# Layer 0's score maxima read from SBUF, and a probability chain cut in three, in a two-layer cross-attention kernel

## The chip, the cores and the metric

The kernel runs on one core of a Trainium2 chip. A core has five engines that run their own instruction streams: TensorE (PE, matrix products; its weight loads, PEld, are listed apart), VectorE (DVE), ScalarE (ACT), GpSimd (POOL) and SyncE (SP, which here issues nearly all DMAs). They share SBUF, the working memory. PE writes its products to PSUM[...], which VectorE and ScalarE read. The metric is the time of one execution on the device, in microseconds; lower is better.

## The reference

Two layers of cross-attention in float32 over x of shape (4, 512, 320), with a context of 1024 tokens of width 512, and 20 heads of width 16. In layer 0 the last four context tokens are "ip" tokens with their own weights:

```python
scores_t = einsum('bhsd,bhtd->bhst', q, k_t) * attn_scale     # 1020 text tokens
probs_t  = softmax(scores_t, axis=-1)
text_out = einsum('bhst,bhtd->bhsd', probs_t, v_t)
attn_scores = einsum('bhsd,bhnd->bhsn', q, k_ip) * attn_scale # 4 ip tokens
qsem  = _l2norm(einsum('bhst,bte->bhse', probs_t, text_ehs))
sem   = einsum('bhse,bne->bhsn', qsem, _l2norm(ip_ehs))
probs_ip = softmax(attn_scores + SEM_SCALE * sem, axis=-1) * spatial_mask
out = (text_out + einsum('bhsn,bhnd->bhsd', probs_ip, v_ip)) @ W_out + b_out + residual
```

Layer 1 takes that output as its hidden states. It attends to 77 text tokens and, in a second softmax, to the other 947 tokens, adds both results, projects, and adds bias and residual.

The large term of layer 0 is the norm in `_l2norm`: for each query and head the vector probs_t @ text_ehs of 512 numbers is needed to get the sum of its squares. The kernel gets these vectors with a product scheme of seven block products per pair of heads instead of eight (one Strassen step: blocks "11", "21", "t1", "t2", "22", "t3", "t4").

## The kernel before

**Units of work.** A turn is one batch and one tile of 128 query rows: 16 turns. A turn has five groups of four heads: 80 groups, numbered `gi`. A group has two units, one for each pair of heads. A unit runs `part0` to `part3`, and behind each part there is a stop. So a group has eight stops, k = 0 to 7. At each stop other work is slipped in between the products of layer 0: one piece from the queues `sub`, `late` or `proj` (function `item`), at stops 2, 4, 5 and 6 a step of layer 1, at stop 2 the function `max0` of the next group, and at stops 5 to 7 pieces of the next group's exponentials (`end_stop`).

**The scores of layer 0.** At stops 0 and 1 of group gi, `fill0(gi + 1, k)` makes the next group's scores, half of the context tokens each time (c = 0, then c = 1). `fill` takes two PSUM tiles `sc` of two banks each, one for each pair of heads. 32 small products fill both: four at a time, two into each tile. Then, for each tile, ScalarE copies the scores to an SBUF tile e (line 476), and VectorE takes the maxima over the four context tiles (lines 477 and 478), so that 128 maxima per query are left. The maxima read the PSUM tile. The pool of the `sc` tiles has two of them, and layer 1's scores (`mx`, `ex`) use the same two. So each fill waits until both tiles of the use before are read. Two engines that read one bank are kept apart by the framework, one after the other. For c = 1 the last four tokens are left out of the maxima and the remaining tile is added by two further instructions.

At stop 2 `max0` turns the maxima with PE, finishes them, and sends the negated maxima through DRAM to all partitions (tile `bc`). `do_exp` adds them to e on VectorE, ScalarE takes the exponential (line 710), and GpSimd prepares a difference.

**Products around the fills.** `part0` writes banks b1 and b2; ScalarE copies b1 (tile `p`, line 804), VectorE adds b2 to it (`c`) and ScalarE sums the squares of `c` (`junk`, line 790). `part1` makes a product into bank b3, VectorE copies that (`p5`; the profile leaves out numbers of buffers, so it is `p` as well, on the row of a VectorE COPY `p<-b`), and a second product goes to b1. `part2` accumulates a further product on b3: PE has to wait for the copy `p5`.

**Order.** All of PE's instructions and those of VectorE that go through `vec` are kept in the order of the program. What goes through `nc.vector`, `nc.scalar` and `nc.gpsimd` is placed by the framework's planner, which has a model of times of its own.

**The end of a turn.** Behind the eighth stop of a turn's fifth group `finish` runs. It loads x, and computes the probabilities of the ip tokens: the sums' reciprocal `r`, scaled outputs `o` and similarities `sem`, the squared norm `n2`, its root on ScalarE (`n1`), and then a softmax over four tokens with an Exp on ScalarE (`pe`), 16 VectorE and 2 ScalarE instructions in all. [...]the trace shows table loads at both. VectorE's part goes through `nc.vector`, in one piece. Then `late` gets two empty pieces and four further ones, one for each of the next stops: `turn_ip` (turns `pe` with PE), `add_ip`, `turn_out` and `multiply`, which starts layer 1 of this turn.

Of the kernel before, what the change touches and what calls it, by code (L numbers as in the profile page):

```python
# [14 lines left out]
AF = mybir.ActivationFunctionType  # L15
ALU = mybir.AluOpType
AX = mybir.AxisListType
# [3 lines left out]
P = 128  # L21
B, S, C = 4, 512, 320
T, E = 1024, 512
H, D = 20, 16
NIP = 4
# [15 lines left out]
V0W = D + NIP + 1  # L41
# [5 lines left out]
TH = TT // 2  # L47
# [3 lines left out]
SEM_SCALE = 0.5  # L51
EPS2 = 1e-24
# [3 lines left out]
def xattn_pair(ctx_stack: ExitStack, tc: tile.TileContext, a: dict, out: bass.AP):  # L56
    nc = tc.nc
# [18 lines left out]
    def mm(out, lhsT, rhs, start, stop, on=False):  # L76
        tc.keep_in_program_order(nc.tensor.matmul(out, lhsT=lhsT, rhs=rhs, start=start, stop=stop, skip_group_check=on))  # L77
# [11 lines left out]
    vec = InOrder(nc.vector)  # L89

    def tr(out, in_, ident):
        tc.keep_in_program_order(nc.tensor.transpose(out, in_, ident))  # L92
# [5 lines left out]
    def tp(name):  # L98
        turn_of[0] += 1
        if idle[0] and turn_of[0] % 4:  # L100
            return ps_qs.tile([P, 512], F32, tag=f"qs{turn_of[0] % 4 - 1}", name=name)
        return ps_tp.tile([P, 512], F32, tag="tp", name=name)
# [31 lines left out]
    spat = cst.tile([P, ST], F32, name="spat")  # L134
# [5 lines left out]
    def load_x(b, s, ns, pl, tag):  # L140
        t = pl.tile([P, ns, C], F32, tag=tag, name=f"{tag}_{b}_{s}")
        nc.sync.dma_start(t, a["x"][b, s * P : (s + ns) * P, :].rearrange("(t p) c -> p t c", p=P))
        return t
# [87 lines left out]
    def zero_below(t):  # L231
        nc.gpsimd.memset(t[64:, NC - 1, :], 0.0)
        return t
# [208 lines left out]
    late = deque()  # L442
# [21 lines left out]
    def fill(c, m, name):  # L464


        ps = [ps_sc.tile([P, 2, 512], F32, tag="sc", name=f"sc{name}_{c}_{i}") for i in range(2)]
        for j in range(TH):
            t = (TH * c + j) * P
            for r in range(4):  # L470
                mm(ps[r // 2][:, r % 2, j * P : (j + 1) * P], kq[0][0][32 * r : 32 * r + D, t : t + P],
                   qq[0][0][32 * r : 32 * r + D, :], True, True)
        e = []
        for i in range(2):
            e.append(ep.tile([P, 2, TH, P], F32, tag="e0", name=f"e{name}_{c}_{i}"))
            nc.scalar.copy(e[i].rearrange("p h t s -> p (h t s)"), ps[i].rearrange("p h n -> p (h n)"))  # L476
            vec.tensor_reduce(m[:, c, 2 * i : 2 * i + 2, :],
                                    ps[i][:, :, 0 : (TH - c) * P].rearrange("p h (t s) -> p h s t", s=P), AX.X, ALU.max)
        return e


# [181 lines left out]
    def fill0(gi, c):  # L663
        if gi >= len(G):
            return
        name = f"0_{gi}"
        if c == 0:
            ms[gi] = big.tile([P, 2, 4, P], F32, tag="m0", name=f"m{name}")
        e = fill(c, ms[gi], name)
        for i in range(2):  # L670
            es[gi, i, c] = e[i]
        if c:

            m = ms[gi]
            vec.tensor_tensor(m[:, 0], m[:, 0], m[:, 1], ALU.max)
            for i in range(2):
                x = m[:, 0, 2 * i : 2 * i + 2, :]
                vec.scalar_tensor_tensor(x, x, drop[:, 0:1], e[i][:, :, TH - 1, :], ALU.add, ALU.max)
            if gi + 1 < len(G):
                turn, g = G[gi + 1]  # L680
                load_quad(0, zs[TURNS[turn][0]], turn, g)
# [149 lines left out]
    def finish(turn):  # L831
        b, s = TURNS[turn]
        w, z, name = state.pop(turn), zs[b], f"0_{turn}"

        def small(tag, shape):
            return (st2 if tag in ("pT", "oT") else big).tile(shape, F32, tag=tag, name=f"{tag}_{name}")

        def wide(t, n=NIP):
            return t.unsqueeze(2).to_broadcast([P, H, n])

        z.xr[turn] = xr = load_x(b, s, 1, st3, "xr")
        nc.gpsimd.tensor_tensor(xr, xr, bo[0].unsqueeze(1).to_broadcast([P, 1, C]), ALU.add)
        pv, ss, ips = w["pv"], w["ss"], w["ips"]
        r = small("r", [P, H])
        nc.vector.reciprocal(r, pv[:, :, V0W - 1])
        o = small("o", [P, H, D])
        nc.vector.tensor_tensor(o, pv[:, :, 0:D], wide(r, D), ALU.mult)
        sem = small("sem", [P, H, NIP])
        nc.vector.tensor_tensor(sem, pv[:, :, D : D + NIP], wide(r), ALU.mult)

        n2 = small("n2", [P, H])
        nc.vector.tensor_tensor(n2, ss[:, :, 0], ss[:, :, 1], ALU.add)
        nc.vector.tensor_tensor(n2, n2, r, ALU.mult)
        nc.vector.tensor_tensor(n2, n2, r, ALU.mult)
        nc.vector.tensor_scalar(n2, n2, EPS2, None, ALU.max)
        n1 = small("n1", [P, H])
        nc.scalar.activation(n1, n2, AF.Sqrt)
        rn = small("rn", [P, H])
        nc.vector.reciprocal(rn, n1)
        nc.vector.tensor_tensor(sem, sem, wide(rn), ALU.mult)  # L860
        pe = small("pe", [P, H, NIP])
        nc.vector.scalar_tensor_tensor(pe, sem, SEM_SCALE, ips, ALU.mult, ALU.add)
        mx = small("mx", [P, H])
        nc.vector.tensor_reduce(mx, pe, AX.X, ALU.max)
        nc.vector.tensor_tensor(pe, pe, wide(mx), ALU.subtract)
        nc.scalar.activation(pe, pe, AF.Exp)
        sums = small("sums", [P, H])
        nc.vector.tensor_reduce(sums, pe, AX.X, ALU.add)
        re = small("re", [P, H])
        nc.vector.reciprocal(re, sums)  # L870
        nc.vector.tensor_scalar(re, re, spat[:, s : s + 1], None, ALU.mult)
        nc.vector.tensor_tensor(pe, pe, wide(re), ALU.mult)
        of2, box = o.rearrange("p h d -> p (h d)"), {}

        def turn_ip():
            pt = tp(f"pt_p_{name}")
            tr(pt[: H * NIP, 0:P], pe.rearrange("p h n -> p (h n)"), ident)
            box["pT"] = small("pT", [H * NIP, P])
            vec.tensor_copy(box["pT"], pt[: H * NIP, 0:P])

        def add_ip():
            pt = tp(f"pt_ip_{name}")
            mm(pt[:, 0:C], box["pT"], z.vip, True, True)
            vec.tensor_tensor(of2, pt[:, 0:C], of2, ALU.add)

        def turn_out():
            pt = tp(f"pt_o_{name}")
            for c, (c0, n) in enumerate(CK):
                tr(pt[:n, c * P : (c + 1) * P], of2[:, c0 : c0 + n], ident)
            box["oT"] = zero_below(small("oT", [P, NC, P]))  # L890
            vec.tensor_copy(box["oT"][:, 0:2].rearrange("p c s -> p (c s)"), pt[:, 0 : 2 * P])
            vec.tensor_copy(box["oT"][:64, 2, :], pt[:64, 2 * P : 3 * P])

        def multiply():
            pt = tp(f"pt_y_{name}")
            for c in range(NC):
                mm(pt[:, 0:C], box["oT"][:, c, :], wo0[:, c, :], c == 0, c == NC - 1)
            vec.tensor_tensor(xr[:, 0, :], pt[:, 0:C], xr[:, 0, :], ALU.add)
            layer1(turn)


        late.extend([lambda: None] * 2 + [turn_ip, add_ip, turn_out, multiply])


    z, (turns, scores, layer0, rest) = projections(0)
# [11 lines left out]
    for g in range(HG):  # L917
        for r in range(4):
            c = 64 * g + D * r
# [51 lines left out]
    for gi, (turn, g) in enumerate(G):  # L971
        b, s = TURNS[turn]
        n = gi % NQ
        ending[0] = gi == len(G) - 1
        if n == 1 and b + 1 < B:
            zs[b + 1], steps = projections(b + 1)
            proj.extend(steps)
        if n == NQ - 2:
            while proj:
                proj.popleft()()  # L980
        for i in range(2):
            u = units.pop((gi, i))
            for k, part in enumerate((u.part0, u.part1, u.part2, u.part3)):
                part()
                stop(gi, 4 * i + k)
                if k == 2:
                    ahead(gi + i, 1 - i)
            for c in range(2):
                es.pop((gi, i, c))
        if g == HG - 1:  # L990
            finish(turn)
# [29 lines left out]
```

## Time and profile before

| | before |
|---|---|
| median of 3 runs | 3784.29 us (3783.63 to 3785.22) |
| the profiled execution | 3784.95 us, its span 3783.2 us |
| PE busy | 3547.9 us (94%) |
| PEld busy | 2826.8 us (75%) |
| DVE busy | 2080.8 us (55%) |
| ACT busy | 1498.8 us (40%) |
| POOL busy | 1012.3 us (27%) |
| mean granted PE clock | 0.958 of full speed |
| copies of the scores (line 476) | 320, 1.01 us each |
| DMA queue of SyncE | 30% of 16 engines' span |

The span runs from the first to the last instruction; the execution is longer by 1.75 us. An engine's busy share is an average over the whole span. An idle engine costs nothing unless the others wait for it, so the rows of interest are those that tell what ended an engine's idle time. The clock column tells which share of its full speed PE was granted: it is 1.00 or 0.50 in every stretch.

### The profile page before, as it was taken

To read this page: it belongs to the slowest core of one execution; us is meant where nothing else is said; L and a number is where in the kernel's file an instruction comes from. 1 tells how busy PE (TensorE), PEld (TensorE's weight loads), DVE (VectorE), ACT (ScalarE), POOL (GpSimd) and SP (SyncE) were. 2 spreads that over 40 slices of the span, in tenths; PEclk is the share of its full clock that TensorE was granted. 3 is DMA by queue.
4 is the path that set the end of the run, shared out by engine and by line. 5 is a ranking of instruction groups with operands and counts; after the bars stand their busy time and mean duration, and the time that the engine had idled before them with its cause. 6 is when DMAs were issued, how large, how long until landed. Compare 5 with 4: busy or idle time off the path is not lost.

```text
span 3783.2 us, 74188 instructions
## 1 busy us (share of the span) xinstructions
PE 3547.9 (94%) x29060; PEld 2826.8 (75%) x29060; DVE 2080.8 (55%) x3795; ACT 1498.8 (40%) x2824; POOL 1012.3 (27%) x1039
## 2 busy tenths in 40 slices
PE   7799999999999999999999999999999999999976
PEld 5677777777787777777777787777777777777765
DVE  2344455566554654556665554556665665665544
ACT  1233334344443433434443443444444444444432
POOL 1222222233222222223322222222322322332210
PEclk9899999999999999999999999999999999999986
DMA  6444332222334233222234433222232222222211
GB/s 180 106 125 125 71 83 39 49 39 48 84 87 102 60 97 89 50 63 40 44 80 104 101 69 95 62 58 45 46 79 48 44 41 51 41 44 38 46 34 26
DMA packets 704986, 258.76 MB, mean 68 GB/s; under 512 B 571024, under 2 KB 679024, under 8 KB 704640
## 3 DMA queue, kind: packets, MB, share of 16 engines
q1 hardware_dynamic: 704464, 253.82, 30.0%
q8 instruction: 232, 3.80, 0.4%
q14 instruction: 114, 0.93, 0.1%
q10 hardware_dynamic: 176, 0.20, 0.0%
HBM read 213.51 MB, written 40.33 MB: 67 GB/s over the span
## 4 chain that ended last, share of the span: by engine, by line
PE 79%; DVE 12%; ACT 3%; DMA 3%; issue 2%; SPq 1%; POOL 0%; DVEq 0%; ACTq 0%; POOLq 0%
PE b L77 47%; PE ex L77 6%; PE pv L77 5%; DVE m L87 5%; PE pt_k L77 4%; PE sc L77 4%; DVE e L87 4%; PE mx L77 4%; PE pt_v L77 3%; PE pt_y L77 2%; PE pt_q L77 2%; PE mx L92 1%; ACT e L710 1%; ACT e L476 1%; DVE c L87 1%
## 5 line engine op out<-in xcount | busy, mean ns | idle before, releaser
L77 PE MATMUL b<-xv_t,e 128*128 128x277 f32 x2560 | 675.7, 407 | 1.3 <-DVE c L87 1.3
L77 PE MATMUL b<-xv,e 128*128 128x277 f32 (+1 forms) x2560 | 653.4, 408 | 10.7 <-ACT e L710 10.7
L77 PEld LDWEIGHTS b<-xv,e 128*128 128x128 f32 x2560 | 480.1, 190 | 145.0 <-ACT e L710 10.9
L77 PEld LDWEIGHTS b<-xv_t,e 128*128 128x128 f32 x2560 | 486.8, 195 | 117.4 <-DVE c L87 4.6
L710 ACT ACTIVATE e<-e 128x1024 f32<-128x1024 f32 x320 | 338.2, 1057 | 468.0 <-DVE e L87 467.8
L805 POOL TENSOR_TENSOR e<-e,s 128x512 f32<-128x512 f32 x160 | 223.8, 1398 | 1071.2 <-PE b L77 1071.2
L87 DVE TENSOR_REDUCE m<-sc 128x256 f32<-128x1024 f32 (+1 forms) x320 | 338.0, 1087 | 267.7 <-ACT e L476 267.7
L87 DVE TENSOR_REDUCE m<-mx 128x2 f32<-128x870 f32 (+1 forms) x320 | 363.7, 1137 | 100.9 <-PE ex L77 92.5
L529 ACT ACTIVATE e<-ex 128x1024 f32<-128x1024 f32 x320 | 325.7, 1018 | 235.9 <-PE ex L77 235.9
L790 ACT ACTIVATE junk<-c 128x256 f32<-128x256 f32 x480 | 198.7, 414 | 513.1 <-DVE c L87 505.1
L77 PE MATMUL ex<-qa,kq 19*128 19x128 f32 x5120 | 383.3, 290 | 6.8 <-DVE qa L87 5.9
L77 PE MATMUL mx<-kq,qq 16*128 16x512 f32 x1280 | 365.2, 661 | 21.4 <-DVE m L87 15.2
L476 ACT COPY e<-sc 128x1024 f32<-128x1024 f32 x320 | 307.4, 1012 | 196.0 <-PE sc L77 194.8
L87 DVE TENSOR_TENSOR e<-e,bc 128x1024 f32<-128x1024 f32 x320 | 368.9, 1173 | 9.5 <-DMA bc<-zd 9.5
L77 PE MATMUL b<-xs,e 128*128 128x256 f32 x1280 | 366.8, 436 | 0.0
L712 POOL TENSOR_TENSOR e<-e 128x512 f32<-128x512 f32 x160 | 205.4, 1284 | 594.5 <-ACT e L710 594.4
L87 DVE TENSOR_TENSOR c<-b,p 128x256 f32<-128x256 f32 x320 | 134.1, 419 | 408.0 <-PE b L77 369.2
L77 PEld LDWEIGHTS ex<-qa,kq 19*128 19x128 f32 x5120 | 321.5, 192 | 13.6 <-DVE qa L87 5.4
L77 PE MATMUL b<-xs_t,e 128*128 128x256 f32 x1280 | 319.6, 393 | 8.0 <-POOL e L805 8.0
L77 PE MATMUL sc<-qq,kq 16*128 16x128 f32 x5120 | 221.8, 299 | 93.3 <-DVE m L87 93.3
L77 PE MATMUL b<-xs_t,s 128*128 128x256 f32 x1280 | 303.2, 380 | 2.1 <-ACT p L804 2.1
L77 PEld LDWEIGHTS b<-xs,e 128*128 128x128 f32 x1280 | 259.0, 212 | 56.6 <-issue 4.4
(192 smaller groups left out, 4221.8 us busy)
## 6 DMA issues: line engine op xcount, KB each, us to landing
kq<-kd SPq DMA_DIRECT2D x640, 64.0 KB
v1q<-v1d SPq DMA_DIRECT2D x80, 373.5 KB
bc<-zd SPq DMA_DIRECT2D x80, 256.0 KB
xv<-v0d SPq DMA_DIRECT2D x480, 42.0 KB
xv_t<-v0d SPq DMA_DIRECT2D x320, 42.0 KB
L_xattn_W_k<-in_L_xattn_W_k_dram SPq DMA_DIRECT2D x13, 640.0 KB
L_xattn_W_v<-in_L_xattn_W_v_dram SPq DMA_DIRECT2D x13, 640.0 KB
raw<-in_ctx_dram SPq DMA_DIRECT2D x32, 256.0 KB
```

What stands on the lines that cost most here:

```text
L77: tc.keep_in_program_order(nc.tensor.matmul(out, lhsT=lhsT, rhs=rhs, start=start, stop=stop, skip_group_check=on))
L87: return lambda *args, **kw: keep(getattr(self.engine, name)(*args, **kw))
L92: tc.keep_in_program_order(nc.tensor.transpose(out, in_, ident))
L476: nc.scalar.copy(e[i].rearrange("p h t s -> p (h t s)"), ps[i].rearrange("p h n -> p (h n)"))
L529: nc.scalar.activation(e.rearrange("p i j s -> p (i j s)"), ps.rearrange("p i n -> p (i n)"), AF.Exp)
L710: nc.scalar.activation(flat, flat, AF.Exp)
L712: nc.gpsimd.tensor_tensor(e[:, 1], e[:, 1], e[:, 0], ALU.subtract)
L790: nc.scalar.activation(junk, x, AF.Square, accum_out=self.w["ss"][:, self.h + r, k : k + 1])
L805: nc.gpsimd.tensor_tensor(self.e("11"), self.e("11"), self.s2, ALU.add)
```

## The change

Two edits. In `fill` the maxima read e, the copy in SBUF that ScalarE has just made, and no longer the PSUM tile; the elements and their order are the same. In `finish` the chain is cut in three: `norms` runs at once, `exps` at the next stop and `shares` at the one behind it, in the places of the two empty pieces. All of the chain's VectorE instructions go through `vec` now, so they hold their place in the program's order, and the root's input is computed before `o` and `sem`.

```diff
@@ fill
-            vec.tensor_reduce(m[:, c, 2 * i : 2 * i + 2, :],
-                                    ps[i][:, :, 0 : (TH - c) * P].rearrange("p h (t s) -> p h s t", s=P), AX.X, ALU.max)
+            vec.tensor_reduce(m[:, c, 2 * i : 2 * i + 2, :], e[i][:, :, 0 : TH - c].rearrange("p h t s -> p h s t"), AX.X,
+                              ALU.max)
@@ finish
-        nc.vector.reciprocal(r, pv[:, :, V0W - 1])
-        nc.vector.tensor_tensor(o, pv[:, :, 0:D], wide(r, D), ALU.mult)
-        nc.vector.tensor_tensor(sem, pv[:, :, D : D + NIP], wide(r), ALU.mult)
-        nc.vector.tensor_tensor(n2, ss[:, :, 0], ss[:, :, 1], ALU.add)
...
-        nc.vector.tensor_tensor(pe, pe, wide(re), ALU.mult)
+        def norms():
+            vec.reciprocal(r, pv[:, :, V0W - 1])
+            vec.tensor_tensor(n2, ss[:, :, 0], ss[:, :, 1], ALU.add)
+            vec.tensor_tensor(n2, n2, r, ALU.mult)
+            vec.tensor_tensor(n2, n2, r, ALU.mult)
+            vec.tensor_scalar(n2, n2, EPS2, None, ALU.max)
+            nc.scalar.activation(n1, n2, AF.Sqrt)
+            vec.tensor_tensor(o, pv[:, :, 0:D], wide(r, D), ALU.mult)
+            vec.tensor_tensor(sem, pv[:, :, D : D + NIP], wide(r), ALU.mult)
+        def exps():
+            vec.reciprocal(rn, n1)
+            vec.tensor_tensor(sem, sem, wide(rn), ALU.mult)
+            vec.scalar_tensor_tensor(pe, sem, SEM_SCALE, ips, ALU.mult, ALU.add)
+            vec.tensor_reduce(mx, pe, AX.X, ALU.max)
+            vec.tensor_tensor(pe, pe, wide(mx), ALU.subtract)
+            nc.scalar.activation(pe, pe, AF.Exp)
+        def shares():
+            vec.tensor_reduce(sums, pe, AX.X, ALU.add)
+            vec.reciprocal(re, sums)
+            vec.tensor_scalar(re, re, spat[:, s : s + 1], None, ALU.mult)
+            vec.tensor_tensor(pe, pe, wide(re), ALU.mult)
...
-        late.extend([lambda: None] * 2 + [turn_ip, add_ip, turn_out, multiply])
+        norms()
+        late.extend([exps, shares, turn_ip, add_ip, turn_out, multiply])
```

More of the change, by code (lines that the diff above doesn't have):

```diff
@@ L844, in finish @@
         r = small("r", [P, H])
-        nc.vector.reciprocal(r, pv[:, :, V0W - 1])
         o = small("o", [P, H, D])
-        nc.vector.tensor_tensor(o, pv[:, :, 0:D], wide(r, D), ALU.mult)
         sem = small("sem", [P, H, NIP])
-        nc.vector.tensor_tensor(sem, pv[:, :, D : D + NIP], wide(r), ALU.mult)
         n2 = small("n2", [P, H])
-        nc.vector.tensor_tensor(n2, ss[:, :, 0], ss[:, :, 1], ALU.add)
-        nc.vector.tensor_tensor(n2, n2, r, ALU.mult)
-        nc.vector.tensor_tensor(n2, n2, r, ALU.mult)
@@ L855, in finish @@
-        nc.vector.tensor_scalar(n2, n2, EPS2, None, ALU.max)
         n1 = small("n1", [P, H])
-        nc.scalar.activation(n1, n2, AF.Sqrt)
         rn = small("rn", [P, H])
-        nc.vector.reciprocal(rn, n1)
-        nc.vector.tensor_tensor(sem, sem, wide(rn), ALU.mult)
         pe = small("pe", [P, H, NIP])
-        nc.vector.scalar_tensor_tensor(pe, sem, SEM_SCALE, ips, ALU.mult, ALU.add)
         mx = small("mx", [P, H])
-        nc.vector.tensor_reduce(mx, pe, AX.X, ALU.max)
-        nc.vector.tensor_tensor(pe, pe, wide(mx), ALU.subtract)
@@ L866, in finish @@
-        nc.scalar.activation(pe, pe, AF.Exp)
         sums = small("sums", [P, H])
-        nc.vector.tensor_reduce(sums, pe, AX.X, ALU.add)
         re = small("re", [P, H])
-        nc.vector.reciprocal(re, sums)
-        nc.vector.tensor_scalar(re, re, spat[:, s : s + 1], None, ALU.mult)
-        nc.vector.tensor_tensor(pe, pe, wide(re), ALU.mult)
+        def norms():
[7 more added lines that the diff above has]
+            vec.tensor_tensor(sem, pv[:, :, D : D + NIP], wide(r), ALU.mult)
```

## The prediction

> **What bounds it now.** I read the busy shares first: TensorE (PE) is busy 94% of the span, VectorE (DVE) 55%, ScalarE (ACT) 40%. So the few places where PE stands still decide, and I went to the groups of instructions and their idle time. PE's longest wait by far is in front of the layer-0 score matmuls, and VectorE's maxima of those scores end it:
>
> ```profile
> L87 DVE TENSOR_REDUCE m<-sc 128x256 f32<-128x1024 f32 (+1 forms) x320 | 338.0, 1087 | 267.7 <-ACT e L476 267.7
> ...
> L77 PE MATMUL sc<-qq,kq 16*128 16x128 f32 x5120 | 221.8, 299 | 93.3 <-DVE m L87 93.3
> ```
>
> The last field is idle time and what ended it. The maxima wait for ACT's copy of the same scores: two readers of one bank follow each other, copy first. PE's 93.3 us is two fifths of all that it isn't busy (3783.2 - 3547.9 = 235 us). Going through the timeline fill by fill, all of it is at stop 1 (second fill, c = 1), in 34 of 80 groups: 15 first groups after a turn's end (60.7 us), 18 others (32.3 us), and 0.3 us at the start. An ordinary one:
>
> ```profile
> 2701.52 1.90 ACT L476 COPY e<-sc 128x1024 f32<-128x1024 f32 x2
> ...
> 2702.55 2.35 DVE L87 TENSOR_REDUCE m<-sc 128x256 f32<-128x1024 f32 x2 [1.39 <-ACT e L476]
> ...
> 2703.82 0.49 PE L77 MATMUL sc<-qq,kq 16*128 16x128 f32 x4 [1.08 <-DVE m L87]
> 2704.82 0.41 DVE L87 COPY p<-b 128x256 f32<-128x256 f32 x1
> ...
> 2704.96 1.16 PE L77 MATMUL sc<-qq,kq 16*128 16x128 f32 x28 [0.64 <-DVE m L87]
> ...
> 2706.05 3.17 PE L77 MATMUL b<-xs,e 128*128 128x256 f32 x8
> ```
>
> PE was ready at 2702.74 and got through the fill at 2706.05, 3.31 us later. Note the p copy of part1 (p5, bank b3) right behind the maxima. The chain of waits runs through just such places.
>
> **Maxima, price of one.** 1.216 us for 1024 elements, 0.957 for 768[...]. From SBUF no large reduce is in the trace. Near rows: the SBUF pair m<-m, 512 elements, 692 ns[...]; a SBUF shuffle of 256 takes 438 ns, 442 beside GpSimd, so one input doesn't queue behind GpSimd. I take the same price.[...] Here each element lies 512 bytes after the last[...]. The rows for a strided and a contiguous read of 20 elements:
>
> ```profile
> L845 DVE RECIPROCAL r<-pv x16: 263/266/278, 369.8 to 3645.3; 128x20 f32<-128x20 f32 x16
> ```
> ```profile
> L859 DVE RECIPROCAL rn<-n x16: 262/278/280, 374.0 to 3648.1; 128x20 f32<-128x20 f32 x16
> ```
>
> A step of 84 bytes costs nothing (266 against 278 ns median[...]). The row decides[...].
>
> **Maxima, what is gained.** The banks come free when the second copy ends, 2703.42, not at 2704.90. The fill runs 2703.47 to 2704.60. Then the next product, b<-xs,e into b3, needs the p copy to have read b3, and that copy stands in VectorE's fixed order behind both maxima: 2705.23. So b starts at 2705.29, not 2706.05: 0.76 us, half of what the wait suggests. **The wait moves, from sc to b behind the p copy.** The same arithmetic (fill start = later of ready and copy end; b start = later of fill + 1.13 and p copy end + 0.06) for each of the 33: 16.0 us over the 18 ordinary ones, 23.2 us over the 15 turn ends, together 39. In the other 46 groups the p copy is early by at least 0.43 us, nothing changes.
>
> **Clock.** A stall costs twice here: after it PE runs at half clock.
>
> ```profile
> 2706.70:2710.10 3.40, 3.40 (x10) 2.59 (x9) 2.93 (x4) 1.28 (x2) 0.00 (x0) 0.50 0.25 68
> 2742.30:2745.70 3.40, 3.40 (x27) 2.76 (x29) 2.69 (x3) 1.73 (x3) 1.18 (x1) 1.00 0.03 8
> ```
>
> These are stretches of the stalled group and of its neighbour; the column before the last two is the granted clock.[...] By the trace 12 of the 15 are followed by 3.4 us at 0.50, 1.7 us lost each, 20 us in all; the trace decides. Afterwards such a group idles 0.73 + 0.64 = 1.37 us. Single stalls of 1.27, 1.28 and 1.38 us kept the clock (at 701.6, 2010.2, 602.9), one of 1.51 lost it (2315.2). I take 8 of the 12 as saved: 13 us, ends 0 and 20.
>
> **The chain.** Same 16 x (16 DVE, 2 ACT) instructions, no DMA moved. Now at a turn's end (ACT alone):
>
> ```profile
> 2819.67 1.28 ACT L857 ACT_TABLE_LOAD   x1
> 2820.97 0.22 ACT L857 ACTIVATE n<-n 128x20 f32<-128x20 f32 x1
> 2821.20 1.28 ACT L866 ACT_TABLE_LOAD   x1
> 2822.96 0.27 ACT L866 ACTIVATE pe<-pe 128x80 f32<-128x80 f32 x1 [0.48 <-DVE pe L865]
> 2823.14 1.91 ACT L476 COPY e<-sc 128x1024 f32<-128x1024 f32 x2
> ```
>
> VectorE runs the chain from 2818.21 to 2824.36, 1.55 us of it waiting for the root, and only then c and pv of part0, the maxima and the p copy (to 2827.37). The copies, whose scores were ready at 2818.1, stand behind both table loads. After: norms (1.5 us) to 2819.7 or so, c and pv to 2820.5 while the root loads; rn waits until 2821.2, exps end near 2822.9; shares (1.1 us) go behind the p copy and are hidden, as VectorE waits over 2 us there for the second fill. The new wait blocks the maxima behind rn; they need the copies anyway. What ACT does is open, since its order isn't kept: the Exp may stand before the two copies (copies end 2825.3, p copy 2827.2: 0.2 us better than the maxima alone give), between them (2826.95: 0.45 us), or behind (copies end 2823.7, maxima from 2822.95, p copy 2825.75: 1.65 us). The middle is likeliest: PE issues sc right behind the product that c reads, so the scores are there about when c is, and the Exp needs another 1.3 us of VectorE. The second wait, of shares for the Exp (ended by 2825.3 in each order), has the second fill's maxima behind it, which come later anyway. 15 x 0.45 = 7 us; ends 3 and 25. The loads: a Copy directly behind the root (at 372 us) needed none; for a Square no row tells, so 0 to 16 x 1.28 = 20 us; I take 0, since the Exp reloads anyway. PE's idle at turn ends stays near 4 us, and so do most of the 6.8 us half-clock stretches; I count 3 of 15 shortened by 1.7: 5 us, up to 25 in the good order. At the very end the qa add no longer stands behind the chain (PE waited 3.63 us there at 3648 to 3652): 2 us.
>
> **Sum.** 39 + 13 + 7 + 5 + 2 = 66. The profiled execution took 3784.95 us (span 3783.2 and 1.75 around), the median is 3784.29: 3784.3 - 66 = 3718.
>
> **Rivals.**
> - Copies before the Exp at turn ends: 39 + 20 + 25 + 25 + 2 = 111, 3673. For: scores ready 5 us before they are copied. Against: Exp comes first in the program. Chance 0.2.
> - The wait only moves: b stalls behind the p copy, the clock drops as before, the chain gives nothing; 39 alone, 3745. For: total idle per stalled group falls only from 1.73 to 1.37. Against: the three stalls that kept the clock. 0.22.
> - Slower:[...] It decides from 0.59 us more per maximum (39 / 33 / 2). The rows at 84 bytes[...] speak against. With its milder forms, and a square that reloads tables: 0.12.
> - No change, gain given back at turn ends: 0.03.
> - The forecast: 0.43, its own range 3700 to 3735.
>
> 0.2% is 7.6 us, about what can be told from no change. Faster 0.85, same 0.03, slower 0.12. The range leaves out the slow case and the best tail: 3664 to 3768.
>
> **What would show it.** Right: sc no longer idle behind DVE m but, for about a third of the time, behind ACT e; a new b <- DVE p wait of some 0.6 us in 30 places; maxima from e still at 1.2 and 0.96 us; the rn wait (18.6 us) smaller; fewer 0.50 stretches. Wrong: a maximum over 1.8 us, half-clock time not below 290 us (321 now), copies at turn ends later than 5 us behind the scores, or more than 32 table loads in the chain.

## The result, and the profile after

| | before | after |
|---|---|---|
| median, 11 runs each | 3784.29 us (3781.61 to 3792.54) | 3806.94 us (3792.76 to 3815.05) |
| the profiled execution, span | 3784.95, 3783.2 us | 3792.76, 3790.7 us |
| clock in the profiled execution | 0.958 | 0.960 |

The changed kernel is slower: 1.0055 times the time before, 95% interval 1.0041 to 1.0068. That is 21 us more, where 66 us less had been forecast. The profiled execution of after is the quickest of its eleven. The other ten show granted clocks from 0.952 to 0.958, so the trace explains the first 8 us of the loss. The rest goes with the clock, though no trace of those ten is kept: at a mean of 0.955 PE spends 9% of the time at half speed, at 0.960 8%. One per cent of 3800 us is 38 us at half speed, and 19 us of work lost.

The page of after, busy row and groups by line (busy us, mean ns | idle before it, what ended it):

```profile
PE 3526.4 (93%) x29060; PEld 2813.5 (74%) x29060; DVE 2198.0 (58%) x3795; ACT 1501.1 (40%) x2824; POOL 1014.4 (27%) x1039
...
L87 DVE TENSOR_REDUCE m<-e 128x256 f32<-128x1024 f32 (+1 forms) x320 | 459.4, 1476 | 169.8 <-ACT e L476 168.8
...
L77 PE MATMUL b<-xs,e 128*128 128x256 f32 x1280 | 360.1, 430 | 81.8 <-DVE p L87 55.6
```

VectorE executes the same 3795 instructions and is busy 117 us longer. The maxima alone take 121 us more, 459.4 against 338.0. With the two shapes kept apart, first before, then after:

```profile
L87 DVE TENSOR_REDUCE m<-sc 128x256 f32<-128x1024 f32 x160 | 188.3, 1218 | 106.1 <-ACT e L476 106.1
L87 DVE TENSOR_REDUCE m<-sc 128x256 f32<-128x768 f32 x160 | 149.7, 957 | 161.5 <-ACT e L476 161.5
```
```profile
L87 DVE TENSOR_REDUCE m<-e 128x256 f32<-128x1024 f32 x160 | 301.5, 1926 | 123.5 <-ACT e L476 123.5
L87 DVE TENSOR_REDUCE m<-e 128x256 f32<-128x768 f32 x160 | 157.9, 1027 | 46.3 <-ACT e L476 45.3
```

A maximum over four tiles takes 1.93 us from SBUF, where it took 1.22 from the bank; over three tiles it takes 1.03 instead of 0.96. So the loss is in one of the two shapes, and it isn't a general price of SBUF.

PE's waits of after (us in total, times, longest):

```profile
PE b L77 <- DVE p L87: 55.6, 43, 3.5
PE sc L77 <- ACT e L476: 27.9, 40, 2.0
PE b L77 <- DVE sums L87: 21.7, 12, 2.1
...
PE b L77 <- ACT p L804: 10.7, 9, 1.2
```

The wait of sc for the maxima (93.3 us) is gone, and a wait of sc for ACT's copies is left at 30% of it. But the product b behind the p copy now waits 77 us, the first and third rows together. The third row names `sums`, the first instruction of the chain's third piece. It is the same place at turn ends: VectorE's copy stands right ahead of `sums` there, and PE begins 0.10 us after the copy, before `sums` ends. Releasers are inferred, and one looks at the times before believing a name:

```profile
2834.69 0.42 DVE L87 COPY p<-b 128x256 f32<-128x256 f32 x1
2835.02 0.23 DVE L87 TENSOR_REDUCE sums<-pe 128x20 f32<-128x80 f32 x1
...
2835.21 3.75 PE L77 MATMUL b<-xs,e 128*128 128x256 f32 x8 [1.60 <-issue]
```

The ordinary group that the prediction worked through, on the timeline of after (start, duration, engine, idle before it):

```profile
2707.19 1.89 PE L77 MATMUL b<-xs_t,s 128*128 128x256 f32 x8
...
2707.86 1.91 ACT L476 COPY e<-sc 128x1024 f32<-128x1024 f32 x2
2708.89 3.74 DVE L87 TENSOR_REDUCE m<-e 128x256 f32<-128x1024 f32 x2 [1.39 <-ACT e L476]
...
2709.82 1.16 PE L77 MATMUL sc<-qq,kq 16*128 16x128 f32 x28 [0.32 <-ACT e L476]
...
2712.55 0.41 DVE L87 COPY p<-b 128x256 f32<-128x256 f32 x1
...
2713.11 3.32 PE L77 MATMUL b<-xs,e 128*128 128x256 f32 x7 [2.12 <-DVE p L87]
```

The fill gets its banks at once, 0.32 us late instead of 1.73. Then PE stands 2.12 us before b. From being ready for the fill (2709.08, the end of the first row) to the start of b it takes 4.03 us, where it took 3.31. The products of b last 3.3 us, where eight take 2.0 at full speed; the stretch behind the stall shows a granted clock of 0.50 (the column before the last two):

```profile
2713.60:2716.40 2.80, 2.80 (x8) 2.20 (x7) 2.73 (x5) 0.00 (x0) 0.00 (x0) 0.50 0.26 54
```

I measured this interval in all 80 groups of both traces. The 18 ordinary stalled groups lose 8.5 us in sum. Of the 46 groups without a stall before, 25 now have one, of 0.71 us in the median: 16.8 us. The 15 turn ends gain 20.0, the first group 0.7. Together 4.5 us are lost. The wait for ACT's copy p adds 8.6 us (10.7 against 2.1), and half-speed time falls from 320.8 to 308.6 us, worth some 6. That makes 7 us, about the 7.5 between the two spans.

ACT at a turn's end, after:

```profile
2824.66 1.06 ACT L710 ACTIVATE e<-e 128x1024 f32<-128x1024 f32 x1 [3.24 <-DVE e L87]
2825.74 1.28 ACT L863 ACT_TABLE_LOAD   x1
2827.03 0.22 ACT L863 ACTIVATE n<-n 128x20 f32<-128x20 f32 x1
2827.16 0.37 ACT L804 COPY p<-b 128x277 f32<-128x277 f32 x1
...
2828.55 1.28 ACT L873 ACT_TABLE_LOAD   x1
2829.84 0.27 ACT L873 ACTIVATE pe<-pe 128x80 f32<-128x80 f32 x1
2830.02 1.91 ACT L476 COPY e<-sc 128x1024 f32<-128x1024 f32 x2
```

Both loads still stand ahead of the copies of the scores. New is that the copy p of part0, which PE's next product needs, now stands behind the root's load. The copies begin 5.6 us behind their scores in 10 of the 15 turn ends, where 5.0 was the rule before.

### The profile page after: what moved, and what is told of

Its sections match the earlier page's. It is cut to its first block, busy times and chain, and to the rows that moved or that the text cites. A ratio compares the mean times of both kernels' runs of the same rounds, so it can differ in the third digit from the quotient of the medians.

```text
span 3790.7 us, 74186 instructions
## 1 busy us (share of the span) xinstructions
PE 3526.4 (93%) x29060; PEld 2813.5 (74%) x29060; DVE 2198.0 (58%) x3795; ACT 1501.1 (40%) x2824; POOL 1014.4 (27%) x1039
## 4 chain that ended last, share of the span: by engine, by line
PE 72%; DVE 15%; ACT 5%; DMA 3%; issue 3%; SPq 1%; POOL 0%; ACTq 0%; DVEq 0%; POOLq 0%
PE b L77 45%; DVE m L87 8%; PE ex L77 6%; PE pv L77 5%; DVE e L87 4%; PE pt_k L77 4%; PE mx L77 4%; PE pt_v L77 3%; PE pt_y L77 2%; ACT e L476 2%; PE sc L77 2%; PE mx L92 1%; ACT e L710 1%; PE pt_q L77 1%; ACT junk L790 1%
## 5 line engine op out<-in xcount | busy, mean ns | idle before, releaser
L87 DVE TENSOR_REDUCE m<-e 128x256 f32<-128x1024 f32 (+1 forms) x320 | 459.4, 1476 | 169.8 <-ACT e L476 168.8
L77 PE MATMUL b<-xs,e 128*128 128x256 f32 x1280 | 360.1, 430 | 81.8 <-DVE p L87 55.6
L77 PE MATMUL b<-xs_t,s 128*128 128x256 f32 x1280 | 304.2, 380 | 10.7 <-ACT p L804 10.7
L77 PEld LDWEIGHTS b<-xs_t,s 128*128 128x128 f32 x1280 | 243.3, 191 | 48.0 <-ACT p L804 14.7
```

The source lines that it names most:

```text
L87: return lambda *args, **kw: keep(getattr(self.engine, name)(*args, **kw))
```

## The experiments

The first question was what brings the loss: the price of the strided maximum, which the p copy queued behind two of them pays twice, or the order in which VectorE and ACT now do their work. Ratios are to the runs of the kernel before on the same chip.

**Each edit alone.** The first kernel has only the edit in `fill`:

```diff
-            vec.tensor_reduce(m[:, c, 2 * i : 2 * i + 2, :],
-                                    ps[i][:, :, 0 : (TH - c) * P].rearrange("p h (t s) -> p h s t", s=P), AX.X, ALU.max)
+            vec.tensor_reduce(m[:, c, 2 * i : 2 * i + 2, :], e[i][:, :, 0 : TH - c].rearrange("p h t s -> p h s t"), AX.X,
+                              ALU.max)
```

> Only the first edit: maxima from SBUF, the chain as before. Theory 'price' (a maximum over four tiles costs 1.92 us from SBUF and 1.22 from the banks, and the p copy that PE waits for stands behind two of them): slower than before by 20 to 45 us, since the ordinary groups lose 25.8 us as in the changed kernel and the turn ends gain next to nothing without the split chain. Theory 'order' (the chain held in program order is what costs): 35 to 70 us faster than before, as forecast for the maxima alone.

The second has only the edit in `finish`:

```diff
+        norms()
+        late.extend([exps, shares, turn_ip, add_ip, turn_out, multiply])
```

> Only the second edit: chain in three pieces, maxima from the banks. Theory 'price': faster than before by 20 to 60 us, as the turn ends gain (19.8 us in the changed kernel in spite of the dear maxima, 15 x 1.4 us more without them) and the ordinary groups are as before. Theory 'order': slower than before, by 10 to 40 us.

The maxima alone: 3814.3 us, ratio 1.0080 (1.0067 to 1.0092), 30 us slower. The chain alone: 3768.0 us, ratio 0.9958 (0.9945 to 0.9972), 16 us faster, a little less than the 20 to 60 expected under "price". So the whole loss is the first edit's. On top of it the second still gives some 9 us (1.0055 for both against 1.0080). PE's waits with the maxima alone:

```profile
PE b L77 <- DVE p L87: 83.3, 55, 3.6
PE sc L77 <- ACT e L476: 37.4, 40, 2.4
```

The two rows make 120.7 us, in place of the 93.3 us of one wait before.

**The same edit with another instruction.** If the price decides, the change's own idea must pay once the maximum is cheap. Here the maxima still read e, in the same place in the order, but as maxima of two tiles at a time; `m[:, 1]` serves as scratch at c = 0.

```diff
-            vec.tensor_reduce(m[:, c, 2 * i : 2 * i + 2, :], e[i][:, :, 0 : TH - c].rearrange("p h t s -> p h s t"), AX.X,
-                              ALU.max)
+            mi = m[:, c, 2 * i : 2 * i + 2, :]
+            if c == 0:
+                h2 = m[:, 1].rearrange("p (h k) s -> p h k s", h=2)
+                vec.tensor_tensor(h2, e[i][:, :, 0:2], e[i][:, :, 2:4], ALU.max)
+                vec.tensor_tensor(mi, h2[:, :, 0], h2[:, :, 1], ALU.max)
+            else:
+                vec.tensor_tensor(mi, e[i][:, :, 0], e[i][:, :, 1], ALU.max)
+                vec.tensor_tensor(mi, mi, e[i][:, :, 2], ALU.max)
```

> The changed kernel, with each maximum from SBUF made of two pairwise maxima over contiguous runs (512 and 256 elements for four tiles, 256 and 256 for three) in place of one strided reduce. Theory 'price': 0.69 + 0.45 = 1.15 us for four tiles, so the p copy comes as early as from the banks or a little earlier; about the forecast, 3690 to 3740 us, and PE's wait for DVE p about 0.6 us in some 30 places. Theory 'order': no faster than 3790 us.[...]

3740.1 us, ratio 0.9887 (0.9874 to 0.9901): 43 us faster than before. One maximum over four tiles takes 0.82 and 0.45 us in the mean, 1.27 together, near the 1.22 from the bank. (The first takes 0.69 us in the median, but 39 of 160 took longer, up to 1.76; what held them up was not tested.) Timeline of an ordinary group:

```profile
2675.16 0.98 DVE L87 TENSOR_TENSOR m<-e 128x512 f32<-128x512 f32 x1 [1.39 <-ACT e L476]
...
2676.10 1.16 PE L77 MATMUL sc<-qq,kq 16*128 16x128 f32 x28 [0.33 <-ACT e L476]
...
2677.77 0.42 DVE L87 COPY p<-b 128x256 f32<-128x256 f32 x1
...
2678.34 1.97 PE L77 MATMUL b<-xs,e 128*128 128x256 f32 x8 [1.08 <-DVE p L87]
```

The wait has moved from sc to b here as well, at 0.33 + 1.08 = 1.41 us in place of 1.73, and b runs at full speed. With the price put right, the sign of the change turns.

**The same maxima, behind the p copy.** This tries the other cause, the place behind which the p copy waits. The maxima keep their slow form, but those of the first fill are put off to stop 1, where they are issued behind part1's p copy.

```diff
+    def maxima(gi, c):
+        for i in range(2):
+            vec.tensor_reduce(ms[gi][:, c, 2 * i : 2 * i + 2, :],
+                              es[gi, i, c][:, :, 0 : TH - c].rearrange("p h t s -> p h s t"), AX.X, ALU.max)
...
+        if c == 0:
+            owed.append(gi)
...
+            while owed:
+                maxima(owed.pop(), 0)
+            maxima(gi, 1)
...
+        if k == 1 and owed:
+            maxima(owed.pop(), 0)
```

> The changed kernel, the strided maxima of a group's first fill put behind part1's p copy in VectorE's order (at the start of stop 1). Theory 'price': the dear maxima stand in nobody's way up to the turning of the maxima at stop 2, PE's 77 us of waiting for DVE p and sums go, leaving the wait for ACT's copies (28 us): 3690 to 3740 us, unless the turning at stop 2 becomes late. Theory 'order': no faster than 3790 us.

3721.1 us, ratio 0.9835 (0.9821 to 0.9848), with maxima of 1.93 us as in after. The product that waited 81.8 us waits no more (group row, shapes apart), and its mean falls from 430 to 405 ns, with a mean granted clock of 0.972 where after has 0.960:

```profile
L77 PE MATMUL b<-xs,e 128*128 128x256 f32 x1280 | 332.8, 405 | 0.1
```

So the slow maximum hurts by the place it stands in. It doesn't vanish from the end, though. The maxima end later, and PE's transposes of them at stop 2 wait:

```profile
L92 PE MATMUL mx<-ident,m 128*128 128x128 f32 x320 | 57.4, 296 | 38.9 <-DVE pT L87 14.0 <-DVE m L87 12.4 <-DVE v L87 4.9
```

It was 21.6 us in after.

**What makes the strided maximum slow.** The kernel before, with 72 maxima of zeros added at its end, each form four times. Two explanations: the step of 512 bytes (then another step is cheap), or the number of places that feed one output (then the step doesn't matter).

```diff
+    cases = [("two", 2, 128), ("three", 3, 128), ("four", 4, 128), ("five", 5, 128), ("six", 6, 128), ("seven", 7, 128),
+             ("eight", 8, 128), ("fourodd", 4, 129), ("fourpair", 4, 130), ("fourline", 4, 132), ("fourtwoline", 4, 136),
+             ("fourlong", 4, 160), ("fourdouble", 4, 256), ("fourhalf", 4, 64), ("fournear", 4, 4), ("fourdense", 4, 1),
+             ("fourbank", 4, 128), ("threebank", 3, 128)]
```

> The kernel before, with 72 added maxima of zeros at its end, four of each of 18 shapes, which nothing reads: over two to eight tiles 512 bytes apart in SBUF; over four tiles at other steps (64, 129, 130, 132, 136, 160, 256 elements; 4 elements; next to each other); over four and three tiles in a bank. The price itself is looked for[...]. Theory 'step' (a stride of 512 bytes is slow in SBUF): all counts slow alike, padded steps fast. Theory 'count'[...]: two and three tiles fast (0.42 and 0.55 us), four slow (near 1.0), and the step doesn't matter. The bank cases: 0.68 and 0.55 us under both.

The second number of a case is the inputs per output, the third the step between them in elements. One tile's instructions (minimum, median, maximum in ns; first and last start; shapes):

```profile
L87 DVE TENSOR_REDUCE two<-probe x4: 361/423/424, 3782.5 to 3783.8; 128x128 f32<-128x256 f32 x4
L87 DVE TENSOR_REDUCE three<-probe x4: 592/593/595, 3784.3 to 3786.2; 128x128 f32<-128x384 f32 x4
L87 DVE TENSOR_REDUCE four<-probe x4: 1017/1018/1019, 3786.8 to 3790.0; 128x128 f32<-128x512 f32 x4
L87 DVE TENSOR_REDUCE five<-probe x4: 1231/1232/1232, 3791.0 to 3794.8; 128x128 f32<-128x640 f32 x4
...
L87 DVE TENSOR_REDUCE fourodd<-probe x4: 1018/1019/1020, 3816.4 to 3819.6; 128x128 f32<-128x512 f32 x4
...
L87 DVE TENSOR_REDUCE fournear<-probe x4: 599/601/605, 3844.2 to 3846.1; 128x64 f32<-128x256 f32 x4
L87 DVE TENSOR_REDUCE fourdense<-probe x4: 419/420/421, 3846.7 to 3848.1; 128x64 f32<-128x256 f32 x4
```

And from a bank (group rows):

```profile
L87 DVE TENSOR_REDUCE fourbank<-bank 128x128 f32<-128x512 f32 x4 | 2.8, 691 | 0.1
...
L87 DVE TENSOR_REDUCE threebank<-bank 128x128 f32<-128x384 f32 x4 | 2.2, 557 | 0.1
```

Two inputs (423 ns for 256 elements) cost no more than four neighbours, which are also 256 elements (420). Three cost 36 ns more than from a bank. Four cost 327 more. From there each further input adds 214 ns for 128 elements, where the fourth from a bank added 134 (691 - 557). Steps of 129, 130, 132, 136, 160 and 256 elements all gave 1018 to 1020. So at these steps it is the count of places, and none of the padded steps helped. Inputs that lie 4 elements (16 bytes) apart are slow as well, 601 ns where neighbours take 420. Why the fourth place costs so much more than the third is open.

**Both remedies.** Pairs, put behind the p copy, with the chain in three pieces (the edit against the kernel with the slow maxima behind the p copy):

```diff
     def maxima(gi, c):
+        m = ms[gi]
         for i in range(2):
-            vec.tensor_reduce(ms[gi][:, c, 2 * i : 2 * i + 2, :],
-                              es[gi, i, c][:, :, 0 : TH - c].rearrange("p h t s -> p h s t"), AX.X, ALU.max)
+            mi, e = m[:, c, 2 * i : 2 * i + 2, :], es[gi, i, c]
...
+                vec.tensor_tensor(h2, e[:, :, 0:2], e[:, :, 2:4], ALU.max)
+                vec.tensor_tensor(mi, h2[:, :, 0], h2[:, :, 1], ALU.max)
```

> Pairwise maxima and the p copy first together, with the split chain. Theory 'price': with the p copy in front of the maxima their price matters only up to stop 2, so 0 to 12 us less than with the p copy first alone (3721), through PE's wait for m at the turning of the maxima (15 us there).

3675.7 us, ratio 0.9729 (0.9715 to 0.9742): it beats both kernels, by 105 and 131 us. The expectation was a miss: I had counted on 0 to 12 us beyond the order alone, and some 40 came by the ratios (45 by the medians). Matched product by product with the run before, 26 us of the 43 between the two traces come where both run at full speed: 14 at the transposes `mx` of the maxima, which the slow maxima had held up, and 12 at b<-xv_t,e, whose wait for VectorE's `c` falls from 4.8 to 1.1 us in all. The other 16 are clock: products at half speed in one run and at full speed in the other. Turn ends idle about as long in both (24.1 and 26.1 us in front of sc and b), but 4 of 15 are followed by half speed here and 11 there.

The traces' clock records show where. In those of before and after the clock changes 99 and 101 times, each time a multiple of 3.413 us after the last, to within 0.001 us: half speed lasts 3.41, 6.83, 10.24 us and so on, except where the record of after ends. Here is one turn end of 1.91 us idle, first with the slow maxima, then with pairs. Each row is one step of 3.41 us: its length, the busy time of PE, PEld, DVE, ACT and POOL, and then the granted clock:

```profile
2979.27:2982.69 3.42, 1.99 (x8) 1.44 (x8) 1.99 (x8) 2.89 (x7) 1.83 (x2) 1.00 0.01 2
2982.69:2986.10 3.41, 1.89 (x33) 1.57 (x34) 2.34 (x2) 2.53 (x5) 0.00 (x0) 1.00 0.00 0
2986.10:2989.51 3.41, 3.41 (x9) 2.66 (x8) 3.31 (x7) 1.62 (x2) 0.00 (x0) 0.50 0.24 66
```
```profile
2946.22:2949.64 3.42, 1.93 (x11) 1.26 (x10) 1.93 (x7) 3.39 (x6) 0.30 (x1) 1.00 0.00 0
2949.64:2953.05 3.41, 2.99 (x39) 2.60 (x38) 3.10 (x10) 2.53 (x4) 0.00 (x0) 1.00 0.08 25
2953.05:2956.46 3.41, 3.23 (x30) 2.42 (x28) 3.31 (x9) 0.29 (x2) 0.00 (x0) 1.00 0.31 71
```

Nine turn ends of each run idle 1.91 us. With the slow maxima all nine lose the clock: PE became ready 0.4 us or 2.4 to 3.4 us into a step. With pairs seven keep it, ready at 1.4 to 2.0 us, and two lose it, ready at 0.7 and 2.8. So at the same length of stall, the place separates the seven from the eleven others in these two traces. With one trace of each kernel it isn't known whether the stalls of other executions lie alike; as far as the runs show, the part of the gain that is clock may be luck.

**The old chain with each form of maxima.** The p-first kernels again, with `finish` as in before:

```diff
-        norms()
-        late.extend([exps, shares, turn_ip, add_ip, turn_out, multiply])
+        late.extend([lambda: None] * 2 + [turn_ip, add_ip, turn_out, multiply])
```

With the slow maxima:

> Strided maxima from SBUF behind the p copy, with the chain of the kernel before. What the split is worth when the maxima are out of PE's way: 15 us (as from the kernel before to the split chain alone) if the gains add up: 3736. If the split only pays where the p copy is late: 3721 to 3726.

With pairs:

> The last kernel of both maxima edits (pairs, put behind the p copy) with the chain of before, in one piece at the turn's end. Theory 'chain neutral': the three pieces gave 15 us alone because they took VectorE's wait for the root out of the way of maxima and p copy; with the p copy ahead of the maxima that cover is had without them, so the time is within 12 us of the one with the pieces (3664 to 3688), with the wait of sc for ACT e about 10 us more and that of b for the ACT copy p about 10 us less. Theory 'chain pays': with short maxima the pieces at stops 1 and 2 no longer delay the transposes of the maxima (the price that hid their gain with long ones), so without them 15 to 30 us come back: 3690 to 3706. Slower than 3706 would speak against both.

With slow maxima 3715.9 us, ratio 0.9828 (0.9815 to 0.9842), not to be told from 0.9835 with the pieces: the gains do not add up, as 3736 would have said. With pairs 3694.2, ratio 0.9766 (0.9753 to 0.9779), so the pieces are worth some 14 us there by the ratios and 18 by the medians, the low end of what the second theory gave. PE's waits with pairs, first with the pieces, then with the old chain:

```profile
PE sc L77 <- ACT e L476: 30.8, 42, 2.7
...
PE b L77 <- ACT p L818: 11.9, 10, 1.2
```
```profile
PE sc L77 <- ACT e L476: 40.1, 42, 2.4
...
PE b L77 <- ACT p L818: 3.2, 2, 2.5
```

What the pieces give at sc they take at b. Idle time is nearly equal, 186.5 and 189.7 us. The gain in these two traces is clock: 194.5 us at half speed against 246.8, which is worth 26 us, all that is between them. (The first is the quickest of its five executions, the second the slowest.) With slow maxima behind the p copy the pieces shared VectorE with them at stops 1 and 2, and the transposes waited 14.0 us for `pT`, 5.9 without the pieces.

**The root too at a later stop.** The p copy behind the root's table load costs 9 us of waits, so I moved `norms` off the turn's end as well, in the kernel with both remedies:

```diff
-        norms()
-        late.extend([exps, shares, turn_ip, add_ip, turn_out, multiply])
+        late.extend([norms, exps, shares, turn_ip, add_ip, turn_out, multiply])
```

> The sixth kernel with the chain's first piece too put off to the next stop, so that part0's copy of bank b1 stands in front of the root's table load on ScalarE and c in front of the chain on VectorE. PE's wait for ACT p (11 us in the changed kernel) goes, and the wait for ACT e at turn ends shrinks: 10 to 25 us less than the sixth kernel; no gain if ScalarE's order puts the table loads in front of the copies all the same.

3736.4 us, ratio 0.9882 (0.9868 to 0.9895): 58 us slower than without this step, a miss. The wait aimed at is gone, but a new one leads the list:

```profile
PE b L77 <- POOL e L819: 43.4, 32, 2.9
PE mx L77 <- DVE m L87: 16.3, 9, 3.0
```

One more item in `late` puts every later piece of a turn one stop on, layer 1's start with them. The wait for GpSimd's addition was 8.0 us in 8 places. Which of the shifted pieces makes it late wasn't followed up.

## Why the prediction was wrong, step by step

**Maxima, price of one: the step that failed.** It took 1.216 us from the row of 20 elements at a step of 84 bytes ("The row decides"). Measured: 1.926 us for four tiles. The row could not decide. It is a RECIPROCAL, and another row of before shows what one takes over 256 elements that lie side by side:

```profile
L87 DVE RECIPROCAL den<-den x80: 1752/1753/1755, 506.3 to 3775.9; 128x256 f32<-128x256 f32 x80
```

A shuffle of 256 takes 438 ns. From 1753 ns for 256 elements and 278 for 20, a reciprocal spends about 6 ns on each element (an estimate), three times the 1.9 ns of the slow maximum, so the row need not show what a read costs. The row also has one input per output and a single run of addresses, while the maximum takes four runs in turn. The shuffle and the pair `m<-m`, the other two rows, had nearer sizes and no jumps. Two places 512 bytes apart, read in turn, cost nothing in the probe (423 ns for 256 elements, 420 for neighbours); three cost 0.07 us in a maximum of 768 elements, four 0.71 in one of 1024. No maximum of before reads places far apart in SBUF, so the price should have stayed an open cost with both signs.

**Maxima, what is gained: the wait right, the gain not reached.** The wait moved to b behind the p copy, as written. With the measured price its arithmetic gives 0.64 + 2 × 0.71 = 2.06 us in the ordinary group; the trace has 2.12. With maxima of 1.27 us the stalls were 1.41 us where 1.37 had been forecast for 1.22. But b began 2.98 us after PE was ready, where 2.55 had been forecast and 3.31 was the time before: 0.33 us gained instead of 0.76. In the group shown, the four instructions in front of the p copy took 2.69 us from the first start to the last end; the two maxima from the banks took 2.35. No run has maxima from SBUF at the forecast price.

**Clock: half speed behind stalls right, the saving half.** It counted on 8 of 12 half-speed stretches saved at 1.37 us. In the pairs run, of 15 ordinary stalls of 1.40 us, 8 are followed by half speed; before, 12 of 15 at 1.73; in after, 10 of 15 at 2.45. So 4 were saved, 7 us instead of 13. The length of a stall does not sort them, as the single stalls of 1.38 and 1.51 us had suggested. Their place in the steps of 3.413 us sorts those of each run. Before, the three that kept the clock began 1.7 to 1.8 us into a step and the twelve others within 0.1 us of its start or after 2.7. In the pairs run the seven that kept it began at 1.2 to 2.7 us, the others before 0.8 or after 2.75; in after the five began at 1.0 to 1.1, the others before 0.9 or after 2.4.

**The chain: the sum near by luck, the path not.** 7 + 5 + 2 = 14 us were forecast on top of maxima from SBUF; 16 came with the chain alone, some 9 on top of the slow maxima. But the Exp stood before the copies, not between them as I took for likeliest. And the copy p behind the root's load wasn't seen: its wait rose from 2.1 to 11.6 us in the run with the chain alone. There sc's wait fell by 17 us (93.3 to 76.0), and half-speed time by 16 (320.8 to 304.8), worth 8. A larger gain and a cost that had been put at nothing cancel, so that the sum fits is luck. There are 35 table loads in all before and after, so the square brought none.

**Sum.** Of the four signs of being wrong, three showed: a maximum over 1.8 us, half-speed time of 308.6 us, copies 5.6 us behind the scores. The fourth did not, with 31 table loads at the chain's two lines.

**Rivals.** The slower one had the decision point: 0.71 us more per maximum is past the 0.59 that it names, by 0.12 × 2 × 33 = 8 us. How much more a maximum would cost, and so the size of the loss, rested on no row of before. Of the 46 groups without a stall 25 lost their slack, at 16.8 us, and none of these was followed by half speed. A chance of 0.12 was too small for a cost that no row showed. "The wait only moves", at 3745, is what the pairs run, with its cheap maxima, came near to, 3740, in its number but not in its parts, as it lets the chain give nothing.

## What to carry to other kernels

Before an operand is moved from one memory to another, the price of the very access pattern has to be known there, above all the number of places that feed one output (here 0.07 us more for three, 0.71 us for four): a few dozen instructions added at the end of a kernel measure it. When a wait is removed, look at what stands behind the same instructions on their engine. Here the short copy behind the maxima decided, and moving it ahead of them gained 65 us even with the slow maxima and the old chain.

## What the runs showed of the hardware that was not expected

A VectorE maximum over four places far apart takes 691 ns for 512 elements from a PSUM bank and 1018 ns from SBUF, whatever the step from 128 to 256 elements; at 4 and 64 elements it is slow as well (601 and 585 ns for 256 elements, where neighbours take 420). Two places take 423 ns for 256 elements, three 593 ns for 384, where a bank takes 557. Two maxima of pairs over 1024 elements take 1.12 us where neither is held up (0.69 and 0.42) instead of 1.93.

Of PE's idle times of one length some were followed by half speed and some were not: stalls of 1.40 us in 8 of 15 places (pairs), of 1.73 in 12 of 15 (before), of 2.45 in 10 of 15 (after), and the stalls of 0.71 us in the median that after added in 25 groups in none. In the clock records of before and after the changes lie multiples of 3.413 us apart, and in each of the three runs the place in these steps at which a stall began sorted the 15, where its length did not.
